# A graph-network kernel whose layer 2 changes its order of rows: products turn two columns, and the scatters move from the layer's input and its first output to its second

## The chip, the cores and the metric

The kernel runs on one core of a Trainium2 chip. The metric is the device time of one execution in microseconds. Three runs of the kernel before gave 706.58, 708.85 and 709.79 us, a median of 708.85.

## The reference

Four graph layers work on 2708 nodes with 128 features each. The adjacency matrix `adj` is sparse: its entries are 0 or between 0.05 and 1, some 9 in a row. Each layer's result is added to its input and normalised.

```python
x = _layernorm(x + _L0_gnn_ref(x, adj, adj, L0_gnn_W, L0_gnn_a))
x = _layernorm(x + _L1_gnn_ref(x, adj, L1_gnn_W, L1_gnn_b))
x = _layernorm(x + _L2_gnn_ref(x, adj, L2_gnn_W, L2_gnn_a))
x = _layernorm(x + _L3_gnn_ref(x, adj, L3_gnn_msg_w, ..., L3_gnn_ln_b))

# layer 1
A_t = A + jnp.eye(n);  D_inv = A_t.sum(axis=1) ** -0.5
return relu((D_inv[:, None] * A_t * D_inv[None, :]) @ (H @ W.T + b))
# layer 2: attention with 4 heads; what is not 1 is masked by -1e9 times its distance from 1
e = (s_i[:, None, :] + s_j[None, :, :]) * scale + ((1.0 - adj) * -1e9)[:, :, None]
out = jnp.einsum('ijh,jhd->ihd', jax.nn.softmax(e, axis=1), xp)
# layer 3
messages = gelu(s[:, None, :] + d[None, :, :] + msg_b)
aggregated = jnp.einsum('ijd,ij->id', messages, adj)
h = gelu(concat([x, aggregated]) @ upd_w.T + upd_b) + x      # then a layernorm of its own
```

With the mask of layer 2 only a row's diagonal and its largest other entry can have a share in the softmax. Layer 3 needs, for every row, all its entries with their columns.

## The kernel before

Rows lie on 128 partitions in 22 blocks (`NB`). There are two orders of rows. In the natural order block b holds rows 128b to 128b+127. In the order of degree the longest rows come first, so that block b needs only `CAPS[b]` slots, from 21 down to 2, 187 in all. `PERM` holds the row at each place, `RANK` the place of each row. `V` holds each row's entries from the largest down, and `LIDX` their columns, both in the order of degree: `V[:, :, 0]` and `LIDX[:, :, 0]` are the largest entry off the diagonal and its column.

The layers before. Layers 0 and 1 stream the dense matrix and multiply it on PE (L753) in two halves each; `search` steps on DVE fill `V` and the indices meanwhile. At the end of layer 1's first half `end1` calls `in_order_of_rows` once. It splits a column table into three bf16 parts (L305 to L309), spreads them over `BLOCK` into `back_b` (L511, one buffer), multiplies by the one-hot `BACK` in 22 small matmuls (L516), and adds up (L520): a table in the order of degree comes out in natural order. It does so for `DS`, which gives `dinv`; then DVE multiplies `H2` by it in two halves (L894), and `H2` is the weight of the second half's products.

The generator `finish` closes groups of four blocks of a layer, spread over the steps of the loop: transposes (L635), activations and residual (L641 to L649), the norm's sums on POOL (L251 to L263), squares and norm on ACT (L257, L267), transposes (L664), a copy, products with `W2` (L678), a copy into `XP` (L684). Then it stores `TA` (the features and one score, for gathering, an ACT queue DMA), and one POOL scatter per block sends whole rows of `XD` (266 words: x, features, scores, the diagonal and degree `DD`) to their places by degree in the DRAM tensor `TS` (L693, 22 scatters).

Layer 2 works in the order of degree in four sets of 6, 6, 6 and 4 blocks. POOL gathers for each block the row of the largest entry's column from `TA` (`ga`, L918, 22 gathers); SP loads `TS` back as `OWN` (L922). `own_scores`, `shares` and `rows2` are DVE work on a set, `squares` and `rows3` ACT and PE work, `roots` DVE. `rows3` gives `yd`, the "d" of layer 3, and 22 POOL scatters (L1052) send it to natural order in `TD`, by `PERM`. `norm3` (L1061) gives `X3`, the layer's output, in the order of degree, which is what layer 3 works in.

Layer 3 goes through the blocks by `TURN`. `gathers` issues one POOL gather per slot from `TD` (L1150, 187 of them) into `G`, which has four buffers. `terms` makes PE's s terms from `X3`; `diagonals` (ACT) makes diagonal matrices of the entries; `messages` adds (DVE, L1179) and applies GELU (ACT); `update` multiplies (PE, L1143). `conditions` is a set of DVE checks that run before the first `terms` on DVE and PE. `X3B` is `X3` plus a bias row (L1097).

What sets the order: each engine has one in-order queue. `pinned(...)` chains the instructions of an engine in the order of the program's text; where it is absent a scheduler may move them. The issue of the indirect DMAs, of gathers and scatters alike, is work of POOL's queue.

Of the kernel before, what the change touches and what calls it, by code (L numbers as in the profile page):

```python
# [24 lines left out]
F32 = mybir.dt.float32  # L25
# [11 lines left out]
P = 128  # L37
# [32 lines left out]
def sparse_path(  # L70
# [130 lines left out]
    LIDX = const.tile([P, NB, SLOTS], U32, name="LIDX")  # L201
    PERM = const.tile([P, NB], U32, name="PERM")
    PERMF = const.tile([P, NB], F32, name="PERMF")

    RANK = const.tile([P, NB], U32, name="RANK")

# [388 lines left out]

    HS = lists.tile([P, NB, D], F32, name="HS")
    TA = dram.tile([NP, D + HEADS], F32, name="TA")
    TS = dram.tile([NP, W_], F32, name="TS")
    H2 = lists.tile([P, NB, D], F32, name="H2")
    with (  # L600
        tc.tile_pool(name="l_nat", bufs=NAT) as nat,
# [26 lines left out]
        def finish(layer, bs, sT):  # L628


            n = len(bs)
            g = slice(bs[0], bs[-1] + 1)
            o = pt.tile([P, BANK], F32, name="o_ps")
            for j in range(n):
                pinned(T_.transpose(o[:, blk(j)], sT[:, blk(j)], ident))  # L635
            yield
            if layer:
                y = sb.tile([P, 4, D], F32, name="y1")
                for j, b in enumerate(bs):

                    pinned(V_.scalar_tensor_tensor(  # L641
                        y[:, j, :], H2[:, b, :], 1.0, o[:, blk(j)], ALU.mult, ALU.add
                    ))
                for j, b in enumerate(bs):
                    pinned(S_.activation(
                        y[:, j, :], y[:, j, :], AF.Relu, scale=dinv[:, b : b + 1]
                    ))
            for j, b in enumerate(bs):
                pinned(V_.scalar_tensor_tensor(  # L649
                    X[:, b, :], y[:, j, :] if layer else o[:, blk(j)],  # L650
                    1.0 if layer else RZ[:, b : b + 1], X[:, b, :], ALU.mult, ALU.add,
                    accum_out=SUM[:, b : b + 1],
                ))
            squares, norm = norm_sums(bs)
            yield
            yield
            squares()
            yield
            yield
            norm()  # L660
            yield
            o = pt.tile([P, BANK], F32, name="o_ps")
            for j, b in enumerate(bs):
                pinned(T_.transpose(o[:, blk(j)], X[:, b, :], ident))  # L664
            yield
            xt = small.tile([P, BANK], F32, name="xt")
            pinned(S_.copy(xt[:, : n * P], o[:, : n * P]))
            yield
            if layer:

                K = D + 2 * HEADS
                ts = []
                for k in range(0, n, 2):
                    m = min(2, n - k)
                    t = pt.tile([P, BANK], F32, name="q_ps")[:, : 2 * K]
                    ts.append((k, m, t.rearrange("p (b k) -> p b k", k=K)))
                    for i in range(m):
                        pinned(T_.matmul(  # L678
                            ts[-1][2][:, i, :], xt[:, blk(k + i)], W2, start=True, stop=True
                        ))  # L680
                yield
                for k, m, t in ts:
                    b = bs[0] + k
                    pinned(S_.copy(XP[:, b : b + m, :], t[:, :m, :]))  # L684
                yield
                yield
                nc.scalar.dma_start(
                    TA[bs[0] * P : (bs[-1] + 1) * P, :].rearrange("(b p) c -> p b c", p=P),
                    XP[:, g, : D + HEADS],
                )  # L690

                for b in bs:
                    i = G_.indirect_dma_start(  # L693
                        TS, bass.IndirectOffsetOnAxis(ap=RANK[:, b : b + 1], axis=0),
                        XD[:, b, :], None,
                    )
                    tc.declare_no_dep(i.ins, group="TS", reason="each row has a place of its own")
                    tc.add_to_no_dep_group("TS", i.ins)
            else:

                t = pt.tile([P, BANK], F32, name="q_ps").rearrange("p (b k) -> p b k", k=D)
                for i in range(n):
                    pinned(T_.matmul(t[:, i, :], ONES, B1, start=True, stop=False))
                    pinned(T_.matmul(t[:, i, :], xt[:, blk(i)], W1, start=False, stop=True))
                yield
                pinned(S_.copy(H2[:, g, :], t[:, :n, :]))
                nc.scalar.dma_start(
                    TH[bs[0] * P : (bs[-1] + 1) * P, :].rearrange("(b p) d -> p b d", p=P),
                    H2[:, g, :],
                )  # L710
            yield
# [161 lines left out]
        for h in range(2):  # L873
# [13 lines left out]
            def end1():  # L887
                if later_half:
                    return
                for _ in passes:  # L890
                    pass
                in_order_of_rows(pt, dinv, DS)
                for g in (slice(0, NB // 2), slice(NB // 2, NB)):
                    pinned(V_.tensor_tensor(  # L894
                        H2[:, g, :], H2[:, g, :],
                        dinv[:, g].unsqueeze(2).to_broadcast([P, NB // 2, D]), ALU.mult,
                    ))
# [5 lines left out]

    TD = dram.tile([NP, D], F32, name="TD")
    late = ctx.enter_context(tc.tile_pool(name="late", bufs=1))
    OWN = late.tile([P, NB, W_], F32, name="OWN")
    X3 = late.tile([P, NB, D], F32, name="X3")
    with (
        tc.tile_pool(name="l2", bufs=1) as one,
        tc.tile_pool(name="l2b", bufs=2) as sb,  # L910
# [4 lines left out]
        for k, bs in enumerate(sets):  # L915
            ga = gas[k] = one.tile([P, len(bs), D + HEADS], F32, name=f"ga{k}")
            for i, b in enumerate(bs):
                pinned(G_.indirect_dma_start(  # L918
                    ga[:, i, :], None, TA, bass.IndirectOffsetOnAxis(ap=LIDX[:, b, 0:1], axis=0)
                ))  # L920
        for k, bs in enumerate(sets):
            nc.sync.dma_start(  # L922
                OWN[:, bs[0] : bs[-1] + 1, :],
                TS[bs[0] * P : (bs[-1] + 1) * P, :].rearrange("(b p) c -> p b c", p=P),
            )
        XO = OWN[:, :, :D]
        PO = OWN[:, :, D : 2 * D]
        SJ = OWN[:, :, 2 * D : 2 * D + HEADS]
# [15 lines left out]
        pinned(S_.copy(WC, t[:, :D]))  # L944

        AM = one.tile([P, NB, 2], F32, name="AM")
        pinned(V_.tensor_scalar(AM[:, :, 1], V[:, :, 0], 1.0, MASK, ALU.subtract, ALU.mult))
        E = one.tile([P, NB, 2, HEADS], F32, name="E")
        mid = [None] * len(sets)

# [90 lines left out]
        def rows3(k):  # L1041
# [4 lines left out]
            for lo, m, z in zs:  # L1046
                for i in range(m):
                    pinned(S_.activation(  # L1048
                        yd[:, lo + i, :], z[:, i, :], AF.Copy, scale=t[:, 3, lo + i : lo + i + 1]
                    ))  # L1050
            for i, b in enumerate(bs):
                i = G_.indirect_dma_start(  # L1052
                    TD, bass.IndirectOffsetOnAxis(ap=PERM[:, b : b + 1], axis=0), yd[:, i, :], None
                )
                tc.declare_no_dep(i.ins, group="TD", reason="each row has a place of its own")
                tc.add_to_no_dep_group("TD", i.ins)

        def norm3(k):
            zs, t = mid[k]
            for i, b in enumerate(sets[k]):  # L1060
                pinned(S_.activation(  # L1061
                    X3[:, b, :], XO[:, b, :], AF.Identity, bias=t[:, 0, i : i + 1],
                    scale=t[:, 3, i : i + 1],
                ))

# [4 lines left out]
        for k in range(last + 1):  # L1070
            rows2(k)
            if k < last:
                shares(k + 1)
            squares(k)
            if k:
                roots(k - 1)
                rows3(k - 1)
        roots(last)
        rows3(last)
        for k in range(last + 1):  # L1080
            norm3(k)

# [2 lines left out]
    with (  # L1087
# [6 lines left out]
    ):  # L1094
        X3B = one.tile([P, NB, D], F32, name="X3B")
        pinned(V_.tensor_tensor(W3[:, D : 2 * D], W3[:, :D], WD, ALU.add))
        pinned(V_.tensor_tensor(X3B, X3, LN_B.unsqueeze(1).to_broadcast([P, NB, D]), ALU.add))  # L1097

        def conditions():

# [2 lines left out]
            count = one.tile([P, NB], F32, name="count")  # L1103
            for b in range(NB):
                pinned(V_.tensor_reduce(count[:, b : b + 1], has[:, b, : CAPS[b]], AX.X, ALU.add))
            pinned(V_.tensor_tensor(count, count, OWN[:, :, W_ - 1], ALU.not_equal))
            pinned(V_.tensor_reduce(FL[:, 4:5], count, AX.X, ALU.max))

            odd = one.tile([P, NB], F32, name="odd")
# [6 lines left out]


            gap = one.tile([P, NB], F32, name="gap")
            pinned(V_.tensor_tensor(gap, V[:, :, 0], OWN[:, :, W_ - 2], ALU.max))
            pinned(V_.tensor_tensor(gap, gap, V[:, :, 1], ALU.subtract))  # L1120
            pinned(V_.tensor_scalar(gap, gap, 4e-7, None, ALU.is_lt))
            pinned(V_.scalar_tensor_tensor(gap, PERMF, float(N), gap, ALU.is_lt, ALU.mult))
# [42 lines left out]
        def diagonals(k):  # L1165
# [3 lines left out]
            W = Ws[k] = wp.tile([P, CAPS[0] + 1, P], F32, name="W")  # L1169
            for s in range(n):  # L1170
                pinned(S_.activation(W[:, s, :], ident, AF.Copy, scale=V[:, b, s : s + 1]))  # L1171
            pinned(S_.activation(W[:, n, :], ident, AF.Copy, scale=OWN[:, b, W_ - 2 : W_ - 1]))

        def messages(k):
            n = CAPS[TURN[k]]
# [79 lines left out]
                tc.add_to_no_dep_group("OUT", i.ins)  # L1255

        gathers(0)
        conditions()
        terms(0)
        diagonals(0)  # L1260
# [538 lines left out]
```

## Time and profile before

| what | value |
|---|---|
| median of 3 runs | 708.85 us |
| the profiled execution, its own time | 709.3 us |
| its span, first to last instruction | 707.5 us |
| busy: PE, DVE, POOL, ACT | 451.2, 393.0, 378.5, 272.4 us |
| mean granted TensorE clock | 0.766 |
| gathers for layer 3 (L1150) | 187, first at 428.80, last at 682.74 us |
| scatters by row (L693, L1052) | 22 of 982 ns and 22 of 1102 ns on POOL |

A group's row gives line, engine, operation, output and input tiles, count, then busy time and the mean of one in ns, then the idle time ahead of it and what ended it. A timeline row gives start and duration in us, and in brackets the idle time of that engine ahead of it and its releaser. For POOL's indirect DMAs the duration is that of making the descriptors; the data land later.

### The profile page before, as it was taken

How to read it: one execution, taken by the hardware profiler on the slowest of the kernel's cores; microseconds unless marked ns; L12 is line 12 of the kernel's file. 1: busy time of each engine (PE TensorE's matmuls, PEld its weight loads, DVE VectorE, ACT ScalarE, POOL GpSimd, SP SyncE). 2: the span in 40 equal slices, each digit the busy share in tenths (PEclk: the TensorE clock that was granted, in tenths of full speed). 3: DMA queues.
4: the chain of work that ended last, by engine and by line, in shares of the span. 5: the costliest groups of instructions: out<-in, count | busy, mean ns of one | idle time of the engine just before them, and what ended most of it. 6: DMA issues, size and time to landing. Idle time of an engine off the chain costs nothing.

```text
span 707.5 us, 8193 instructions
## 1 busy us (share of the span) xinstructions
PE 451.2 (64%) x2565; PEld 301.7 (43%) x2565; DVE 393.0 (56%) x1138; ACT 272.4 (38%) x719; POOL 378.5 (53%) x449
## 2 busy tenths in 40 slices
PE   5889999996164999997511502066646546747461
PEld 5745445663152444464311501055536435545451
DVE  4767999999983856640208834111171251434466
ACT  3145655772330100174411574055335424444330
POOL 7002001221246776036577677777777777777761
PEclk9579999998556999999755555566776857788665
DMA  9968999996294999875254111222122122211210
GB/s 296 406 245 309 415 415 379 324 374 224 101 386 153 419 418 415 311 216 191 85 181 128 42 52 40 53 54 52 52 53 55 53 53 53 53 52 52 54 48 13
DMA packets 44400, 128.68 MB, mean 182 GB/s; under 512 B 7983, under 2 KB 19523, under 8 KB 38716
## 3 DMA queue, kind: packets, MB, share of 16 engines
q0 software_dynamic: 16832, 75.13, 30.2%
q1 hardware_dynamic: 21116, 49.66, 19.7%
q10 hardware_dynamic: 6400, 3.29, 1.7%
q8 instruction: 22, 0.36, 0.2%
q14 instruction: 30, 0.25, 0.1%
HBM read 119.29 MB, written 8.81 MB: 181 GB/s over the span
## 4 chain that ended last, share of the span: by engine, by line
DVE 27%; POOL 24%; PE 19%; issue 14%; DMA 9%; ACT 6%; SPq 0%; POOLq 0%; DVEq 0%; ACTq 0%
POOL G L1150 17%; PE acc L753 12%; DVE IX L580 9%; DVE cand L565 5%; DMA G<-TD,LIDX 4%; PE z L753 3%; POOL ga L918 2%; DMA TOP<-in_high 1%; POOL TS L693 1%; ACT squares L257 1%; PE w_ps L355 1%; ACT XD L267 1%; ACT X L1061 1%; DMA nat<-in_adjo,PERM 1%; POOL ln_r L262 1%
## 5 line engine op out<-in xcount | busy, mean ns | idle before, releaser
L1150 POOL DMA_INDIRECT G<-TD,LIDX x187 | 177.4, 948 | 58.7 <-issue 52.4
L1143 PE MATMUL aT_ps<-W,M 128*128 128x128 f32 x418 | 91.0, 394 | 112.5 <-ACT M L1180 105.1
L1143 PEld LDWEIGHTS aT_ps<-W,M 128*128 128x128 f32 x418 | 80.9, 292 | 126.4 <-ACT M L1180 114.0
L1179 DVE TENSOR_TENSOR M<-G,sd_ps 128x1152 f32<-128x1152 f32 (+11 forms) x22 | 28.3, 1287 | 159.0 <-DMA G<-TD,LIDX 142.8
L753 PE MATMUL acc<-ah,XD 128*128 128x512 f32 (+1 forms) x264 | 113.7, 568 | 1.0 <-ACT XD L626 1.0
L580 DVE FIND_INDEX8 IX<-V,nat 128x8 uint32<-128x2707 f32 x33 | 97.8, 2970 | 0.0
L830 ACT ACTIVATE sign<-ah 128x1536 bf16<-128x1536 f32 (+1 forms) x44 | 57.7, 1327 | 37.1 <-issue 26.8
L753 PE MATMUL acc<-ah,HS 128*128 128x512 f32 x132 | 63.3, 615 | 12.1 <-ACT HS L866 12.1
L753 PEld LDWEIGHTS acc<-ah,XD 128*128 128x128 f32 x264 | 47.9, 196 | 44.5 <-issue 41.4
L536 POOL DMA_INDIRECT nat<-in_adjo,PERM x22 | 21.5, 979 | 81.5 <-DVE IX L580 55.4
L1171 ACT ACTIVATE W<-TAB,V 128x128 f32<-128x128 f32 x187 | 56.8, 390 | 0.0
L558 DVE MAX8 V<-nat 128x8 f32<-128x2707 f32 x12 | 35.7, 2976 | 26.6 <-DMA nat<-in_adjo,PERM 26.6
L1180 ACT ACTIVATE M<-sd_ps 128x128 f32<-128x128 f32 x22 | 6.1, 278 | 113.2 <-DVE M L1179 113.2
L753 PEld LDWEIGHTS acc<-ah,HS 128*128 128x128 f32 x132 | 25.4, 196 | 44.7 <-issue 29.3
L866 ACT ACTIVATE HS<-HS,DS 128x128 f32<-128x128 f32 x22 | 8.4, 399 | 78.0 <-DMA HS<-TH,PERM 48.8
L565 DVE MAX8 cand<-nat 128x8 f32<-128x338 f32 (+3 forms) x88 | 34.3, 461 | 2.8 <-DMA nat<-in_adjo,PERM 2.8
L251 POOL TENSOR_SCALAR ln_a<-SUM 128x4 f32<-128x4 f32 (+1 forms) x12 | 2.9, 238 | 61.1 <-DVE XD L649 33.2
L1250 POOL DMA_INDIRECT out_x<-yo,PERM x22 | 22.1, 1003 | 18.5 <-DVE yo L1229 11.3
L861 POOL DMA_INDIRECT HS<-TH,PERM x22 | 21.0, 957 | 19.6 <-DMA TH<-H 10.1
L1052 POOL DMA_INDIRECT TD<-yd,PERM x22 | 24.2, 1102 | 9.6 <-ACT yd L1048 4.1
L753 PE MATMUL acc<-ah,H 128*128 128x512 f32 (+1 forms) x88 | 28.1, 462 | 0.0
L693 POOL DMA_INDIRECT TS<-XD,RANK x22 | 21.6, 982 | 11.3 <-issue 5.4
(281 smaller groups left out, 862.6 us busy)
## 6 DMA issues: line engine op xcount, KB each, us to landing
ah<-in_adjL SPq DMA_DIRECT2D x22, 768.0 KB, 13.5
ah<-in_adjR SPq DMA_DIRECT2D x44, 330.0 KB, 5.5
TOP<-in_high SPq DMA_DIRECT2D x5, 1354.0 KB, 13.0
ah<-in_adjL SPq DMA_DIRECT2D x22, 256.0 KB, 7.2
G<-TD,LIDX POOLq DMA_INDIRECT x187, 2.5
OWN<-TS SPq DMA_DIRECT2D x3, 798.0 KB, 8.5
TA<-XD ACTq DMA_DIRECT2D x5, 264.0 KB, 2.8
TH<-H ACTq DMA_DIRECT2D x5, 256.0 KB, 10.2
```

What stands on the lines that cost most here:

```text
L558: pinned(nc.vector.max(V[:, b, 0:8], t))
L565: pinned(nc.vector.max(c[:, 8 * k : 8 * k + 8], t[:, at]))
L580: pinned(nc.vector.max_index(IX[:, b, s], V[:, b, s], t))
L693: i = G_.indirect_dma_start(TS, bass.IndirectOffsetOnAxis(ap=RANK[:, b : b + 1], axis=0), XD[:, b, :], None,)
L753: pinned(T_.matmul(acc[i][:, :w], weights[:, n, :], a[:, i * BANK : i * BANK + w], start=n == 0, stop=n == NB - 1,))
L830: pinned(S_.activation(m[:, : hi - lo], a, AF.Sign))
L1052: i = G_.indirect_dma_start(TD, bass.IndirectOffsetOnAxis(ap=PERM[:, b : b + 1], axis=0), yd[:, i, :], None)
L1143: pinned(T_.matmul(t, a, b, start=n == 0, stop=n == len(parts) - 1))
L1150: pinned(G_.indirect_dma_start(G[:, s, :], None, TD, bass.IndirectOffsetOnAxis(ap=LIDX[:, b, s : s + 1], axis=0),))
L1171: pinned(S_.activation(W[:, s, :], ident, AF.Copy, scale=V[:, b, s : s + 1]))
L1179: pinned(V_.tensor_tensor(M[:, :n, :], G[:, :n, :], s_, ALU.add))
L1250: i = G_.indirect_dma_start(out, bass.IndirectOffsetOnAxis(ap=PERM[:, b : b + 1], axis=0), h, None, bounds_check=N - 1, oob_is_err=False,)
```

## The change

Layer 2 works in natural order, directly on `XD`. The scatter into `TS` and the load of `OWN` go. For the gather and the mask, `V[:, :, 0]` and `LIDX[:, :, 0]` are turned into natural order as `V1` and `J1` by two more calls of `in_order_of_rows`. `d` is stored by four plain SP DMAs. The layer's output `X3N`, with the diagonal and degree in two more columns, is scattered to places by degree into `XS` (22 POOL scatters) and loaded back as `X3S` by four SP loads. Four of the scatters, the loads, the sum `X3B` and the conditions come behind `gathers(0)` in the text.

```diff
@@ end of finish(1) @@
-                for b in bs:
-                    i = G_.indirect_dma_start(
-                        TS, bass.IndirectOffsetOnAxis(ap=RANK[:, b : b + 1], axis=0),
-                        XD[:, b, :], None,
-                    )
...
@@ end1 @@
                 in_order_of_rows(pt, dinv, DS)
+                in_order_of_rows(pt, V1, V[:, :, 0])
+                jf = small.tile([P, NB], F32, name="jf")
+                pinned(V_.tensor_copy(jf, LIDX[:, :, 0]))
+                js = small.tile([P, NB], F32, name="up")
+                in_order_of_rows(pt, js, jf)
+                pinned(V_.tensor_copy(J1, js))
...
@@ layer 2 @@
-    OWN = late.tile([P, NB, W_], F32, name="OWN")
-    X3 = late.tile([P, NB, D], F32, name="X3")
+    OWN = XD
+    X3N = late.tile([P, NB, D + 2], F32, name="X3N")
+    X3S = late.tile([P, NB, D + 2], F32, name="X3S")
+    X3 = X3S[:, :, :D]
+    XS = dram.tile([NP, D + 2], F32, name="XS")
+
+    def to_places(bs):
+        for b in bs:
+            i = pinned(G_.indirect_dma_start(
+                XS, bass.IndirectOffsetOnAxis(ap=RANK[:, b : b + 1], axis=0), X3N[:, b, :], None
+            ))
...
+    def from_places():
+        for bs in groups(6):
+            nc.sync.dma_start(
+                X3S[:, bs[0] : bs[-1] + 1, :],
+                XS[bs[0] * P : (bs[-1] + 1) * P, :].rearrange("(b p) c -> p b c", p=P),
+            )
...
-                    ga[:, i, :], None, TA, bass.IndirectOffsetOnAxis(ap=LIDX[:, b, 0:1], axis=0)
+                    ga[:, i, :], None, TA, bass.IndirectOffsetOnAxis(ap=J1[:, b : b + 1], axis=0)
...
-        for k, bs in enumerate(sets):
-            nc.sync.dma_start(
-                OWN[:, bs[0] : bs[-1] + 1, :],
-                TS[bs[0] * P : (bs[-1] + 1) * P, :].rearrange("(b p) c -> p b c", p=P),
-            )
+        pinned(V_.tensor_copy(X3N[:, :, D:], DD))
...
-            for i, b in enumerate(bs):
-                i = G_.indirect_dma_start(
-                    TD, bass.IndirectOffsetOnAxis(ap=PERM[:, b : b + 1], axis=0), yd[:, i, :], None
-                )
+            nc.sync.dma_start(
+                TD[bs[0] * P : (bs[-1] + 1) * P, :].rearrange("(b p) d -> p b d", p=P),
+                yd[:, : len(bs), :],
+            )
...
             if k:
                 roots(k - 1)
                 rows3(k - 1)
+            if k > 1:
+                norm3(k - 2)
+                to_places(sets[k - 2])
         roots(last)
         rows3(last)
-        for k in range(last + 1):
+        for k in (last - 1, last):
             norm3(k)
+        to_places(sets[last - 1])
...
@@ layer 3 @@
         gathers(0)
+        to_places(sets[last])
+        from_places()
+        pinned(V_.tensor_tensor(X3B, X3, LN_B.unsqueeze(1).to_broadcast([P, NB, D]), ALU.add))
         conditions()
         terms(0)
         diagonals(0)
```

In the built program POOL's queue holds, behind the 22 gathers of layer 2: 19 scatters into `XS`, the 21 gathers of `gathers(0)`, 3 scatters, and the rest of the gathers. PE's queue holds the three sets of 22 small matmuls behind each other, with the remaining products of layer 1's first half behind them.

## The prediction

> **What bounds the kernel now.** I read the page's shares and groups first. From 429 us to the end POOL's gathers are back to back, and layer 3 waits for them:
>
> ```profile
> DVE 27%; POOL 24%; PE 19%; issue 14%; DMA 9%; ACT 6%; SPq 0%; POOLq 0%; DVEq 0%; ACTq 0%
> L1150 POOL DMA_INDIRECT G<-TD,LIDX x187 | 177.4, 948 | 58.7 <-issue 52.4
> ```
>
> The idle time ahead of them is "issue", 0.3 us for each: one gather every 1.25 us, 187 of them 234 us. The list of waits says who suffers:
>
> ```profile
> DVE M L1179 <- DMA G<-TD,LIDX: 142.8, 17, 23.7
> ```
>
> So any shift of POOL's stream goes one to one into the end, while a shift of DVE, ACT or PE in layer 3 is free within the slack of four G buffers. The question is only when POOL gets through its work. POOL's timeline around layer 2:
>
> ```profile
> 361.64 0.96 POOL L693 DMA_INDIRECT TS<-XD,RANK  x1 [0.30 <-issue]
> 362.90 1.00 POOL L918 DMA_INDIRECT ga<-TA,LIDX  x1 [0.30 <-issue]
> ...
> 392.01 0.94 POOL L918 DMA_INDIRECT ga<-TA,LIDX  x1 [0.30 <-issue]
> 396.11 1.00 POOL L1052 DMA_INDIRECT TD<-yd,PERM  x1 [3.15 <-ACT yd L1048]
> ...
> 423.52 3.23 POOL L1052 DMA_INDIRECT TD<-yd,PERM  x1 [0.30 <-DMA TD<-yd,PERM]
> 428.80 1.29 POOL L1150 DMA_INDIRECT G<-TD,LIDX  x1 [2.05 <-DVE odd L1110]
> ```
>
> POOL idles 3.15 us before the TD scatters, and 2.05 at their end, where the first gather needs the last scatter landed. The last scatter took 3.23 us instead of 0.96, because DVE ran this from 422.83 to 425.92:
>
> ```profile
> 422.83 3.09 DVE L1097 TENSOR_TENSOR X3B<-X,LN_B 128x2816 f32<-128x2816 f32 x1 [11.35 <-ACT X L1061]
> ```
>
> Last, PE in layer 1's second half, which POOL's TS scatters hold up (ln_v and ln_m stand behind four of them in POOL's queue, ACT's norm waits for ln_m, and PE's transpose for ACT):
>
> ```profile
> 297.59 0.86 PE L516 MATMUL q_ps<-back_b,BACK 128*128 128x66 bf16 x22
> ...
> 300.94 2.38 PE L753 MATMUL acc<-ah,H 128*128 128x512 f32 x8
> ...
> 324.23 1.54 PE L664 MATMUL o_ps<-TAB,XD 128*128 128x128 f32 x4 [2.49 <-ACT XD L267]
> 325.57 4.06 PE L753 MATMUL acc<-ah,H 128*128 128x512 f32 x8
> ...
> 333.03 1.48 PE L664 MATMUL o_ps<-TAB,XD 128*128 128x128 f32 x4 [1.36 <-ACT XD L267]
> ```
>
> **The change, part by part.** I work with the times of the profiled execution (709.3 us, 0.45 above the median of the runs) and follow the start of the first ga gather, A, which is 362.9 before.
>
> *1. Two more products in end1.* back_b has one buffer, so each call must wait for the matmuls of the one before, and PE's queue stands meanwhile, with the rest of the first half's products behind. First call: matmuls end at 298.45, as now (PE, not DVE, is late there; DVE waited 5.8 us for it, so splitting V1 earlier is free). Then DVE: L520 0.3, three L511 at 0.66 (1.8 overlapped): 300.6. PE 0.9: 301.5. DVE: L520 and the cast of LIDX 0.5; the whole split and spread took 290.01 to 292.67, 2.7: 304.7. PE 0.9: 305.6. DVE: L520 and the cast to J1 0.5, H2's first half 1.6: 307.7. PE meanwhile does the six products that lay between 298.29 and 300.94, 2.65: 308.3. The second half starts at 308.3 instead of 300.94: **+7.3**.
>
> *2. TS scatters gone from POOL.* Third group: its squares end at 318.6, ln_v could run then and not at 321.99; PE's idle 2.49 goes and its transposes need 0.6, not 1.5: -3.35. Fourth group likewise: squares done near 324.2 (shifted), the norm ready before PE gets there: the 1.36 and the 0.9 of stretched transposes, -2.2. Fifth group: ln_a waited for eight scatters until 344.63, its sum was ready near 343.4: -1.2. Together **-6.75**. Last, six scatters stood ahead of ga until 362.6, though TA had landed at 358.32 + 1.75 = 360.1: ga can start at 360.2, **-2.7**.
>
> *The clock, where a rule speaks against part 1.* Behind PE's gap of 2.49 us the profile's stretches give a granted clock of 0.88 from 324 to 326 and 0.50 from 326 to 328, and eight products took 4.06 us where they take 2.38: 1.7 us lost. The Trainium skill, "TensorE: Matmul & The Clock Gate", Part 1 (The HAM clock gate), says the clock halves after an idle window of about 3.4 us. Part 1's gaps are 2.2 and 3.2 us, split by a burst: by the rule alone they might pass free; by the row I charge 1.7 for them. The gap at 321.7 goes, with its own slow stretch: -1.5. By the rule +0 and -1.5, by the row +0.2, which I take. A = 360.2 + 7.3 - 6.75 + 0.2 = **361.0**.
>
> *3. Layer 2 up to the first XS scatter.* OWN is no longer loaded: own_scores (waited for 369.64 to 376.78) runs before ga lands, and the set waits for its gathers. The last gather of set 2 lands at A+26.5 (before 391.23, A+28.3: OWN's loads delayed early landings to 5.5 us, later ones were 2.5 to 4.6; 17 pitches of 1.25, 2.1 of contention, 3.1 landing). The DVE stretch from E of set 2 to E of set 3 was 391.35 to 399.50, 8.15: A+34.7. From there to the end of yd of set 1 was 399.50 to 405.2, 5.7: A+40.4. Only behind it on ACT's queue stands norm3(0) (0.49 for one), then a release of 0.36: first scatter at A+41.2 = **402.2**. Before it was yd of set 0, one set earlier, that released POOL at 396.11. POOL's last ga ends near A+29.7, so it idles some 11 us instead of 3.
>
> *4. POOL from there.* 22 XS scatters cost what 22 TD scatters cost (0.96 + 0.30 each, 27.8 together); the 187 gathers are the same. Before, 428.80 - 396.11 = 32.7 us passed until the first gather, 4.9 more than 27.8. After, the first gather waits for no scatter: TD's stores go by SP (free by then; 2.8 us each by the TA row of the same size), the last near A+50, landed by 414, and POOL reaches its first gather near 426. ACT delivers X3N of sets 1 and 2 near A+46 and A+50.5, when POOL is at its 7th (A+48.8) and 13th (A+56.4): hidden. What stays is X3B, now beside gathers. The row says 2.3 us lost. The skill's "Trainium Architecture — The Big Picture", What this means for kernel authors, calls the port that DVE and GpSimd share "an exclusive lock", which would cost up to 3.1, and also the full 0.95 for each sum in layer 2, where the trace shows gathers of 1.33 for 0.94, 0.39 lost. I take the rows, and 0.4 for the sums of the conditions: 2.7. In terms of the first gather: 402.2 + 27.8 + 2.7 = 432.7 against 428.8: **+3.9 us**.
>
> *5. Late consumers.* The 22nd XS scatter ends at 402.2 + 19x1.265 + 21x1.25 + 3x1.265 = 456.3, lands 2.3 later; SP's four loads take perhaps 9 (OWN's, of twice the bytes in as many rows, took 12 for all): 467. Then X3B 3.1, conditions 8.2, PE and ACT 2: the first add near 481 instead of 457.9; gelu must wait for 6.2 us of diagonals that were early before: 487 instead of 460.8. Cover: POOL needs the first G buffer back for its 58th gather, near 504; slack 20 us. ACT's own turns took 11.2, 8.4, 7.6 (460.84 to 472.1, 475.7 to 484.1, 490.56 to 498.1) against POOL's 16.3, 15, 13.8: the lag is made up by the fifth turn; the first stores to out come in the seventh. Costed at nothing; without this cover it would be up to 26 us.
>
> *6. At nothing:* V1, J1, the copy of DD and jc on DVE (before ga lands). SP's from_places stops nothing: its queue is empty behind it.
>
> Sum: A comes 1.9 earlier (+7.3 - 6.75 - 2.7 + 0.2), the first scatter stands 8.0 further behind A (41.2 for 33.2), and 2.2 of wait and lock go (2.7 for 4.9): **+3.9**, 713.2 on the profiled 709.3, 712.8 on the median of 708.85; I say **713**. Break-even is A near 357.
>
> **The rivals.**
> *No change that can be told (within 0.5%, 3.5 us).* The same mechanism with part 1 a little cheaper (2 us if H2 or DVE overlaps better) or ga landing in 2.6. 711. For it: +3.9 lies close to the bound. Chance 0.34.
> *Faster.* PE's gaps in end1 are hidden or the freed POOL speeds layer 1's tail more than I see: the place is A. If the products cost nothing, A is 353.8 and the end 3.3 us earlier, 705.5; it decides where A falls below 353.6 (0.5%). Against: the one back_b buffer and PE's order force the chain, so this needs also an earlier norm3(0). Chance 0.09.
> *Much slower.* The late X3S breaks the cover of part 5: the first add ends after 504, and POOL's gathers stop for a buffer, all that is over 504 being paid. It would need the loads of XS 20 us later. 720 and up. Chance 0.07, within slower.
> *The change doesn't do what it says* at one place: only three of the last four scatters stand behind gathers(0). Worth 1.3 us of lag, nothing at the end.
>
> **How the numbers follow.** Slower by over 0.5% has the forecast's upper part (0.49) and the broken cover: 0.56; within 0.34; faster 0.10. The unknown ends: end1 5.5 to 8.5, clock -1.5 to +2, landing 2.6 to 4.6, the lock 0 to +1, the runs' spread 3 us. That is +3.9 with -6 and +6 or so: 706.5 to 719. The range of slower alone is 712.4 to 719.
>
> **What would show it.** After: two gaps of PE near 299 and 303, the second half's products starting near 308; no idle of PE ahead of L664 near 324 and 333; A near 361; POOL idle some 11 us before the first XS, which ACT's norm3 releases; no wait ahead of the first G gather; a gather of about 3 us where X3B runs; the first add near 481, the adds back on DMA by the fifth turn; the last gather near 686.6. It is wrong if A is below 357, if the first scatter comes within 38 us of A, or if any gather waits for DVE's M.

## The result, and the profile after

On the chip of the first runs the changed kernel takes 712.82 us (median of 7 runs, 712.31 to 715.31) and the kernel before 708.13 (7 runs, 706.30 to 709.79): a ratio of 1.0071, 95% interval 1.0055 to 1.0087. So it is slower, by a little. Predicted were 713.0 and a range of 706.5 to 719. The profiled execution took 712.5 us, its span is 710.5 (709.3 and 707.5 before).

The largest group on the page of the changed kernel, and the line of the list of waits that answers to the one before:

```profile
L1167 POOL DMA_INDIRECT G<-TD,LIDX x187 | 179.7, 961 | 57.0 <-issue 52.1
```

```profile
DVE M L1196 <- DMA G<-TD,LIDX: 98.7, 17, 11.2
```

Layer 3 is still bound by POOL's gathers. DVE waits 98.7 us for them instead of 142.8: its first add now comes 22 us later and finds its gathers landed, and as no gather waits for an add, that costs nothing here. TensorE's timeline at the end of layer 1's first half and in the second half:

```profile
298.03 0.86 PE L519 MATMUL q_ps<-back_b,BACK 128*128 128x66 bf16 x22
300.93 0.87 PE L519 MATMUL q_ps<-back_b,BACK 128*128 128x66 bf16 x22 [2.04 <-DVE back_b L514]
304.91 1.39 PE L519 MATMUL q_ps<-back_b,BACK 128*128 128x66 bf16 x22 [3.11 <-DVE back_b L514]
306.11 3.34 PE L747 MATMUL acc<-ah,HS 128*128 128x512 f32 x4
...
310.14 2.38 PE L747 MATMUL acc<-ah,H 128*128 128x512 f32 x8
...
335.98 1.11 PE L666 MATMUL o_ps<-TAB,XD 128*128 128x128 f32 x4
```

There are the two waits for DVE's lists, then a third product of 1.39 us instead of 0.87, and the second half begins at 310.14 instead of 300.94. The last row is one of the transposes of L666: from 312 to 340 none of them waits any more, now that the scatters of TS are gone. POOL's timeline:

```profile
363.74 1.10 POOL L938 DMA_INDIRECT ga<-TA,J  x1 [7.22 <-issue]
...
404.19 1.00 POOL L915 DMA_INDIRECT XS<-X3N,RANK  x1 [10.62 <-ACT X3N L1075]
...
428.44 0.98 POOL L1167 DMA_INDIRECT G<-TD,LIDX  x1 [0.30 <-issue]
...
468.61 2.84 POOL L1167 DMA_INDIRECT G<-TD,LIDX  x1 [0.30 <-issue]
...
688.67 0.97 POOL L1167 DMA_INDIRECT G<-TD,LIDX  x1 [0.30 <-issue]
...
706.03 0.98 POOL L1267 DMA_INDIRECT out_x<-yo,PERM  x1 [1.06 <-DVE yo L1258]
```

POOL waits 10.62 us for the first X3N (3.15 for the first yd before); nothing holds the first G gather; one gather takes 2.84 us. The last gather is issued at 688.67 instead of 682.74, and the last store of the output at 706.03 instead of 702.44. DVE's two rows that belong to this:

```profile
467.54 3.09 DVE L1277 TENSOR_TENSOR X3B<-X3S,LN_B 128x2816 f32<-128x2816 f32 x1 [57.42 <-DMA X3S<-XS]
...
480.22 2.96 DVE L1196 TENSOR_TENSOR M<-G,sd_ps 128x2688 f32<-128x2688 f32 x1 [1.46 <-PE sd_ps L1160]
```

### The profile page after: what moved, and what is told of

It is laid out like the page before. It is cut to its first block, busy times and chain, and to the rows that moved or that the text cites. A ratio compares the mean times of both kernels' runs of the same rounds, so it can differ in the third digit from the quotient of the medians.

```text
span 710.5 us, 8271 instructions
## 1 busy us (share of the span) xinstructions
PE 442.8 (62%) x2609; PEld 294.3 (41%) x2609; DVE 398.2 (56%) x1159; ACT 271.3 (38%) x719; POOL 357.5 (50%) x427
## 4 chain that ended last, share of the span: by engine, by line
DVE 27%; POOL 23%; PE 19%; issue 13%; DMA 12%; ACT 5%; SPq 1%; POOLq 0%; DVEq 0%; ACTq 0%
POOL G L1167 17%; PE acc L747 12%; DVE IX L583 9%; DVE cand L568 5%; DMA G<-TD,LIDX 4%; DMA TOP<-in_high 3%; PE z L747 3%; POOL ga L938 2%; POOL XS L915 2%; ACT squares L260 1%; ACT XD L270 1%; DVE XD L651 1%; DMA nat<-in_adjo,PERM 1%; POOL ln_r L265 1%; DVE M L1196 1%
## 5 line engine op out<-in xcount | busy, mean ns | idle before, releaser
L1167 POOL DMA_INDIRECT G<-TD,LIDX x187 | 179.7, 961 | 57.0 <-issue 52.1
L1160 PE MATMUL aT_ps<-W,M 128*128 128x128 f32 x418 | 82.5, 366 | 80.5 <-ACT M L1197 73.1
L1160 PEld LDWEIGHTS aT_ps<-W,M 128*128 128x128 f32 x418 | 73.1, 266 | 93.1 <-ACT M L1197 80.8
L1196 DVE TENSOR_TENSOR M<-G,sd_ps 128x1152 f32<-128x1152 f32 (+11 forms) x22 | 28.3, 1287 | 109.0 <-DMA G<-TD,LIDX 98.7
L1277 DVE TENSOR_TENSOR X3B<-X3S,LN_B 128x2816 f32<-128x2816 f32 x1 | 3.1, 3091 | 57.4 <-DMA X3S<-XS 57.4
L938 POOL DMA_INDIRECT ga<-TA,J x22 | 23.4, 1065 | 13.6 <-issue 13.3
```

The source lines that it names most:

```text
L938: pinned(G_.indirect_dma_start(ga[:, i, :], None, TA, bass.IndirectOffsetOnAxis(ap=J1[:, b : b + 1], axis=0)))
L1160: pinned(T_.matmul(t, a, b, start=n == 0, stop=n == len(parts) - 1))
L1167: pinned(G_.indirect_dma_start(G[:, s, :], None, TD, bass.IndirectOffsetOnAxis(ap=LIDX[:, b, s : s + 1], axis=0),))
L1196: pinned(V_.tensor_tensor(M[:, :n, :], G[:, :n, :], s_, ALU.add))
```

## The experiments

The experiments fell on four chips, and that has to be known to read them. On chip A the kernel before takes 707.5 us; on chips B, C and D it takes 789.0, 788.2 and 794.1, and layer 3 is not bound by POOL there. The record of the result above names no chip; the kernel before took 708.1 there, and I count it with A. From set 1 (below) to the first G gather the changed kernel and its variants with the same stages agree to a few tenths on A, B and D (130.4, 130.4 to 130.8, 130.3 us). I therefore compare stages across chips, by distances within one trace, and whole times only on one chip.

These distances carry most of what follows (us; "set 1" is the start of the first 22 matmuls of end1, the same place in all kernels):

| kernel | set 1 to second half | set 1 to first ga | first ga to first scatter of TD or XS |
|---|---|---|---|
| before | 3.35 | 65.31 | 33.21 |
| changed | 12.11 | 65.71 | 40.45 |
| e1, without the products | 3.35 | 56.63 | 40.34 |
| e2, before with the products | 12.46 | 74.49 | 31.64 |
| e5, with the TS scatters | 12.49 | 74.57 | 41.42 |
| e9, gaps filled | 10.25 | 63.59 | 40.43 |
| e4, lists first | 4.75 | 58.09 | 40.27 |
| e3, norms early | 12.52 | 65.74 | 32.21 |

**What the products cost: e1 and e2.** The changed kernel loses them, the kernel before gets them.

```
-                in_order_of_rows(pt, V1, V[:, :, 0])
-                jf = ...; in_order_of_rows(pt, js, jf)
-                pinned(V_.tensor_copy(J1, js))
+                pinned(V_.tensor_copy(V1, V[:, :, 0]))
+                pinned(V_.tensor_copy(J1, LIDX[:, :, 0]))
```

> The changed kernel without its two extra products: V1 and J1 are plain copies of V's and LIDX's first columns, which leaves out turning them into natural order (the outputs are then of other neighbours). Theory (the products stop TensorE, and all behind the first half of layer 1 follows): the second half's products start near 301.4 instead of 310.14, no matmul in the first half runs at half clock, the first ga gather goes out near 355.0 instead of 363.74, and the time is 8 to 9 us below the changed kernel's 712.8: about 704. Rival (the products are covered, and the growth comes from the scatters of X3N): the second half moves, the end does not, 712 to 713.

Measured on chip A: 703.99 us, ratio to before 0.9954 (0.9942 to 0.9966), 8.8 less than the changed kernel, or 8.2 if each is taken against the kernel before that ran beside it. TensorE's timeline of e1, behind set 1 at 296.38:

```profile
297.08 1.96 PE L747 MATMUL acc<-ah,HS 128*128 128x512 f32 x4
...
299.73 2.38 PE L747 MATMUL acc<-ah,H 128*128 128x512 f32 x8
```

The six products behind set 1 follow at once and take 2.65. The second half starts 8.8 us sooner after set 1, and the first ga gather 9.1 sooner. The products are not covered.

> The kernel before with the two extra products added and their results read by nobody. Theory: the second half's products start near 310 instead of 300.94, the scatters of TS and their stalls of TensorE stay as they are and only shift, and the time is 8 to 9 us above 708.1: about 716.5. Rival (the stalls that TS puts on TensorE take up the delay, since POOL's scatters then have more time): plus 0 to 4, 708 to 712.

Measured on chip A: 714.74 us, ratio 1.0097 (1.0075 to 1.0118), 7.2 more than before. The larger stall of TensorE behind the TS scatters is there as before (2.49 us ahead of one transpose). The smaller one shrinks from 1.36 to 0.44, but eight products behind the larger take 4.61 us instead of 4.06. The first ga gather comes 9.2 later after set 1, so the stalls take up nothing in the end, and the rival fails at that place. Of the 9.2, 1.6 are given back in layer 2, perhaps because OWN's loads have more time, and 2.5 in the tail, of which more below. That puts the time under what I expected.

**What the removal of TS was worth: e5.** The 22 scatters stand again where they stood, and nobody reads TS.

> The changed kernel with the 22 scatters of TS put back on POOL where they stood; their result is read by nobody. Theory (their removal was worth 8 to 10 us in the second half of layer 1: 6.6 in TensorE's waits ahead of L664/L666, the rest in front of the ga gathers): the idle ahead of o_ps comes back, the first ga gather goes out 8.5 to 10.5 us later, near 373, and the time is 8 to 10 us above the changed kernel's 712.8, less up to 2.5 that the tail may give back: 719 to 722. Rival (POOL has more idle time in that stage than the scatters need, so their removal saved little): 713 to 716.

Measured on chip B: 801.65 us, ratio to before 1.0220 (1.0139 to 1.0301). The changed kernel has no run on that chip, so whole times cannot be compared, but the stage can be read. TensorE and POOL of e5:

```profile
333.96 1.63 PE L667 MATMUL o_ps<-TAB,XD 128*128 128x128 f32 x4 [2.48 <-ACT XD L270]
```

```profile
372.76 1.00 POOL L947 DMA_INDIRECT ga<-TA,J  x1 [0.30 <-issue]
```

The wait of 2.48 ahead of a transpose is back, six scatters stand ahead of ga again, and set 1 to ga grows from 65.71 to 74.57: 8.9 us, within the theory. e2 and e1 say the same from the other side: 74.49 - 65.71 = 8.8 is the removal in a kernel with the products, 65.31 - 56.63 = 8.7 in one without. Products and removal thus cancel: +9.2 - 8.8, and 0.4 is left at ga.

**Waits, clock and matmuls of the products: e9 and e4.** e9 puts matmuls that nobody reads into the two gaps:

```
                 in_order_of_rows(pt, dinv, DS)
+                filled(pt, 44)          # 128x66, bf16, BACK by itself
                 in_order_of_rows(pt, V1, V[:, :, 0])
+                filled(pt, 70)
```

> The changed kernel with matmuls that nobody reads (44 and 70 of 128x66, bf16) in TensorE's two waits for DVE between the three products, so that TensorE is busy there; everything else is as it was. Theory (the halved clock of 303 to 308 comes from those two waits of 2.0 and 3.1 us): the third product takes 0.87 and not 1.39, the remaining six products of the first half 2.7 and not 4.0, and the second half starts 1.7 to 2.0 us earlier, near 308.3; the time is 0.5 to 2 us lower. Rival (the clock falls for another reason, or waits of this length do not matter to it): the second half starts where it did, near 310.1, or later.

Measured on chip B: 788.96 us, ratio to before 1.0012 (0.9989 to 1.0035); without a run of the changed kernel beside it the whole time says little. The trace says it plainly. The profile's stretches from 302 to 303 and from 306 to 308 of the changed kernel, and then the latter of e9; the granted clock is the third number from the end (from 303 to 306 it is 0.50 and 1.00):

```profile
302.00:303.00 1.00, 0.00 (x0) 0.00 (x0) 0.93 (x5) 0.00 (x0) 0.00 (x0) 0.53 0.00 0
306.00:308.00 2.00, 2.00 (x9) 0.97 (x7) 1.63 (x3) 0.00 (x0) 0.00 (x0) 0.50 0.00 0
```

```profile
306.00:308.00 2.00, 2.00 (x6) 0.89 (x6) 1.90 (x3) 0.73 (x2) 0.00 (x0) 1.00 0.00 0
```

and TensorE's timeline of e9:

```profile
305.15 0.87 PE L526 MATMUL q_ps<-back_b,BACK 128*128 128x66 bf16 x22 [0.98 <-DVE back_b L521]
...
308.52 2.38 PE L754 MATMUL acc<-ah,H 128*128 128x512 f32 x8
```

With the gaps filled, the clock stays at 1.00, the third product takes 0.87 instead of 1.39 and the six products 2.66 instead of 4.03. The second half starts 10.25 after set 1 instead of 12.11 (12.3 to 12.5 in the other kernels of chip B): 1.9 to 2.3 us were the clock. The waits for DVE themselves stay: the second and third set start 2.90 and 6.88 us after set 1 in both kernels.

e4 removes both: all three lists are made first, in back_b and in two buffers of layer 0 that are free by then, and 66 matmuls follow one another.

```
-                in_order_of_rows(pt, dinv, DS)
-                in_order_of_rows(pt, V1, V[:, :, 0])
-                ...
+                in_order_of_rows(pt, signs, (dinv, DS), (V1, V[:, :, 0]), (js, jf))
```

> The changed kernel with the three products in one row: the parts and the lists of all three (three buffers in place of one) are made on DVE before the first of them, where DVE waits for TensorE anyway, and the 66 matmuls follow one another. Theory (what the products cost is TensorE's waits for DVE and the halved clock behind them, not the matmuls): the three sets of 22 take 0.87 each without a gap, the remaining six products 2.65 instead of 4.03, the second half starts near 303 instead of 310.1, and the time is near 706 (6 to 7.5 us less than 712.8). Rival (the matmuls and reductions themselves cost, or the clock halves for another reason): the second half starts after 307, and the time is 710 to 713.

Measured on chip A: 705.11 us, ratio 0.9962 (0.9947 to 0.9977), 7.1 to 7.7 less than the changed kernel. TensorE of e4:

```profile
297.19 0.86 PE L526 MATMUL q_ps<-back_b,BACK 128*128 128x66 bf16 x22
297.89 1.55 PE L526 MATMUL q_ps<-sign,BACK 128*128 128x66 bf16 x44
299.29 1.96 PE L757 MATMUL acc<-ah,HS 128*128 128x512 f32 x4
```

No gap; the second half starts 4.75 after set 1. Of the 8.8 us, 1.4 are the matmuls themselves, 7.4 were one buffer and the order of the instructions. The prediction saw that DVE waits there anyway and counted V1's split as free; e4 shows that all three lists fit into that time once each has a buffer.

**POOL's idle time before XS: e3.**

```
             if k:
                 roots(k - 1)
                 rows3(k - 1)
-            if k > 1:
-                norm3(k - 2)
-                to_places(sets[k - 2])
+                norm3(k - 1)
+                to_places(sets[k - 1])
```

and the last set's scatters stand ahead of the first gathers.

> The changed kernel with the norms of a set written directly behind that set's rows of yd (not one set later), each set's scatters directly behind them, and all 22 scatters of X3N ahead of the first G gather. Theory (the 10.6 us in which POOL waits for the first X3N are a price on the path): the first XS scatter goes out near 396 instead of 404.2, the scatters run on at 1.275 us each, the last G gather and the end come 7 to 8.5 us earlier: about 705. Rival 1 (the last set's rows bound the first G gather, through TD): the first gather waits for TD's landing and the end moves by under 2 us. Rival 2 (the earlier norms on ScalarE delay the next set's squares, and so the last set): gain under 4 us.

Measured on chip A: 705.09 us, ratio 0.9968 (0.9953 to 0.9984), 7.1 to 7.7 less than the changed kernel. POOL of e3:

```profile
395.65 1.17 POOL L915 DMA_INDIRECT XS<-X3N,RANK  x1 [2.58 <-ACT X3N L1075]
...
424.13 0.99 POOL L1165 DMA_INDIRECT G<-TD,LIDX  x1 [0.30 <-issue]
```

The idle time falls from 10.62 to 2.58, first ga to first scatter from 40.45 to 32.21, and the first gather, now behind all 22 scatters, waits for nothing. Both rivals fail: TD had landed, and ScalarE's earlier norms delayed nothing that counts.

**The cover of the late consumers: e6, e7 and f2.** Gathers of later blocks (13, and 25) stand ahead of the last four scatters of X3N.

```
-        gathers(0)
+        for k in range(m + 1):          # m = 1 in e6 and f2, 2 in e7
+            gathers(k)
         to_places(sets[last])
```

> The changed kernel with the second block's 13 gathers moved ahead of the last four scatters of X3N, so that X3S, X3B and the first message add come some 16.5 us later (near 497) while POOL's list of work is as long as before. Theory (the late consumers of X3S are covered, because the fifth block's gathers, which need the first G buffer back, begin only near 505): no change, 712 to 713.5, with the first add near 497. Rival (any delay of the first add is paid at the end, since DVE and ACT run behind the gathers from there on): 5 to 16 us slower.

> As in the case before, but with the second and the third block's gathers (25 in all) ahead of the last four scatters, so that the first add comes some 32 us later, near 512 to 515, behind the moment (near 505) at which POOL wants the first G buffer back. Theory: POOL's first stall in the gathers, 8 to 12 us ahead of the fifth block, and the end later by about that, 720 to 724. Rival 1 (the buffers' slack is larger than the count of them says): no change. Rival 2 (every delay is paid): 30 us slower.

Measured on chip B: 796.14 and 799.22 us, ratios 1.0124 (1.0056 to 1.0192) and 1.0170 (1.0102 to 1.0238). Neither can decide about chip A: POOL stops for DVE's adds on chip B without the edit too (45.7 us in e9). e9, with its filled gaps, took 788.96 there with its first add at 509.55, e6 and e7 7.2 and 10.3 us more with theirs at 518.65 and 519.14, so some lateness is paid on B. But the changed kernel itself was missing, so it and e6 were run once more on one chip.

> The changed kernel itself, beside the kernel before and beside the two kernels that follow, on one chip. The last five runs fell on two chips on which the kernel before takes 788 to 789 us instead of 707.5, because TensorE waits in layer 3 for no cause that the trace shows, 2 to 17 us at a time. If this chip is one of the quick ones: ratio to before 1.007, as at first. If it is one of the slow ones, the gathers do not bound layer 3 there; theory: the ratio is then 1.003 to 1.012, since the first G gather is as late (428.4 against 428.8) but the first message add is 22 us later and is no longer covered.

> The second block's 13 gathers ahead of the last four scatters of X3N, once more, now beside the changed kernel. Quick chip: theory (16 us more of lateness of the first add are covered by the fifth block's gathers beginning only near 505): the same time as the changed kernel within 0.2%; rival (any delay is paid): 5 to 16 us slower. Slow chip, where the consumers and not the gathers bound layer 3: theory: the 16 us are paid in part or whole, 8 to 16 us above the changed kernel; rival (still covered): within 0.3%.

Both fell on chip D: 793.29 us, ratio 0.9987 (0.9961 to 1.0013), and 800.33, ratio 1.0086 (1.0056 to 1.0117). There the first add comes at 510.31 and 517.46. X3B starts 17.0 us later in f2, but the conditions behind it take 10 us less, so that 7.15 are left, and the times are 7.04 apart. In this one pair the lateness is paid in full. POOL of f1, the changed kernel, shows what differs from chip A:

```profile
513.53 0.94 POOL L1167 DMA_INDIRECT G<-TD,LIDX  x1 [9.20 <-DVE M L1196]
```

POOL waits six times, 50.0 us in all, for a G buffer that DVE's add must free. On chip A the same kernel has no such wait. That 16 us more would still be free on chip A was not measured; it stays read from the trace, not shown. My expectation for the ratio on such a chip, 1.003 or more, was wrong: the change costs nothing there that can be told. Why the kernel before is as slow there has no trace, and stays open.

**Both gains together: e8 and f3.** e3's and e4's edits in one kernel.

> The two edits that gained, together: the lists of all three products first (7.7 us less than the changed kernel), and the norms and scatters of X3N one set earlier (7.7 us less). Theory (the two lie in different stages of one path): they add up, 697 to 698.5, which is 1.4% below the kernel before; first ga gather near 355.3, first scatter of X3N near 387, last G gather near 673. Rival (with both, something else is late, such as TD in front of the first gather, or the adds of the messages): 701 to 705.

> The two gaining edits together, once more. Quick chip: 697 to 698.5, ratio to before 0.985 to 0.987, 2.1% below the changed kernel. Slow chip: 0.98 to 0.985 of before, as measured on the first slow one. Rival (the two gains overlap): no better than either edit alone, 0.996.

Measured: 774.07 us on chip C, ratio 0.9832 (0.9792 to 0.9872); 776.73 on chip D, ratio 0.9799 (0.9776 to 0.9823), 16.6 us less than the changed kernel there. It beats the kernel before on both chips, and the changed kernel on D. Its stages up to the scatters add up as they should, on chip D 58.11 from set 1 to ga and 32.41 from ga to the first scatter, each as in e4 and e3 alone. On chip A it was not run: the 697 to 698.5 us expected there are an estimate from 712.8 less twice 7.7. Why it gains as much where POOL is not the bound stays open.

## Why the prediction was right, step by step

**1, the products.** Right. Predicted +7.3 and 1.7 for the clock; e1 and e2 measure 8.8 and 9.1 at the second half and 9.1 to 9.2 at ga. On the clock the row was right: gaps of 2.04 and 3.11 us, with 0.87 us of matmuls between them, gave 0.50 from 303 to 308, and e9 shows that without them it stays at 1.00. But the two gaps are not alike. The 0.53 from 302 to 303 puts the fall at 302.06, when the second gap was only 0.26 us old. So it was the first gap, with these 0.26 us, that brought the clock down, and the rest of the second can only have kept it there. It came back near 308.9 (0.78 from 308 to 310), after 6.8 us. In the kernel before it was down from 325.5 to 329.0 (0.88 from 324 to 326, 0.76 from 328 to 330), 3.4 us. These are two and one of the windows of about 3.4 us that the Trainium skill states ("TensorE: Matmul & The Clock Gate", Part 1, The HAM clock gate: the clock halves after an idle window). So the trace agrees with the window's length; but the 3.4 us ahead of the two falls held 1.1 and 1.3 us of matmuls and transposes, so a window need not be idle throughout.

**2, the removal of TS.** The mechanism was right, the size was not. With the slow stretch that goes with it, I had -6.75 - 2.7 - 1.5 = -10.95; e5 measures -8.9. The failed term is "ga can start at 360.2": 1.75 for TA to land and 0.1 to start. The chain of waits of the changed kernel, just ahead of the first ga gather at 363.74:

```profile
360.15 2.27 DMA TA<-XD
```

TA's last store took 2.27 and POOL started 1.32 after it had landed: 3.59 instead of 1.85, 1.7 of the 2.1 us that were missing. Before, six scatters stood over this time, so no row of POOL before showed how soon it can follow a store. Also, DVE's sums of own_scores now run beside POOL's last ln_m, which takes 0.87 us there instead of 0.19. So A was 363.74 and not 361.0.

**3, layer 2.** Right: A + 40.45 (predicted 41.2), released by ACT's X3N, with 10.62 us of idle time (11).

**4, POOL from there.** Right: from the first scatter to the last gather 284.48 us instead of 286.63, 2.15 less (2.2 predicted), with no wait at the first gather. X3B cost 1.9 us on one gather, where the row had 2.3. But the prediction was wrong to set its rows against "an exclusive lock" (the skill's "Trainium Architecture — The Big Picture", What this means for kernel authors): the rows agree with it. The gather began 1.07 us after X3B and ended 0.82 after X3B's end; before, the scatter began 0.69 after X3B and ended 0.83 after its end. Likewise every gather of layer 2 that began during one of DVE's sums of two tiles ended 0.81 or 0.82 after the sum, in both kernels. So POOL's instruction stood until the sum was over, and its loss depends only on how soon after the sum's start it began: 1.9 us here, 2.5 in e3 and e4, 0.2 to 0.7 beside the sums of 0.95. Neither 3.1 nor 0.95 is due in full, and that 2.3 and 0.4 came near was luck.

**5, the late consumers.** Right on chip A: X3B at 467.54 (467), first add at 480.22 (481), no gather that waits for an add, and an add that waits for its gathers again, 11.21 us, in the fifth turn. On the other chips POOL does stop for a G buffer, as the rival of the broken cover had it; but the kernel before takes as long on D as the changed one, so the change does not pay for it there.

**The sum.** +5.9 us at the last gather, where +3.9 was predicted; 0.4 of it is there before end1. But the end moved by only 3.6, because the tail gave back 2.3 us. So the two misses cancel, and that the measured time lies so near the 713 is luck. The tail was not in my sum. DVE before, then after:

```profile
674.52 0.29 DVE L1206 TENSOR_TENSOR yo<-yo,X 128x128 f32<-128x128 f32 x1 [1.97 <-ACT yo L1196]
...
684.00 0.81 DVE L1179 TENSOR_TENSOR M<-G,sd_ps 128x640 f32<-128x640 f32 x1
```

```profile
678.35 0.28 DVE L1223 TENSOR_TENSOR yo<-yo,X3S 128x128 f32<-128x128 f32 x1
...
687.58 0.81 DVE L1196 TENSOR_TENSOR M<-G,sd_ps 128x640 f32<-128x640 f32 x1
```

The last add but one stands on DVE behind the norms of a set, which begin with this yo; the end follows it by 18.4 us in both kernels. Before, yo waited 1.97 us for ScalarE; after, the wait is gone, because DVE's add ahead of it came later. From the last gather to the last store it is 19.7 us before and 17.4 after, and 18.9 in e1, 18.5 in e3 and e4. e2, with the order of the kernel before, has 17.2: so the shorter tail does not hang on the new order; how gathers and adds fall against each other would explain it, which was not tested. "One to one into the end" holds to about 2.5 us only.

## What to carry to other kernels

A product that waits for another engine's preparation costs the preparation and, where the gaps halve the clock, what runs behind them: make all operands first, in buffers that are free, and let the matmuls follow one another (1.4 us instead of 8.8 here). When a scattered store leaves a queue, ask which transfer it had covered, for that wait appears next; and when it moves behind a later result, look whether that result can be made one set sooner (7.1 to 7.7 us here). What a DVE sum of two tiles costs POOL depends on where POOL's next instruction falls, not on a fixed price. Cover that rests on a bound of one engine is cover only where that engine is the bound.

## What the runs showed of the hardware that was not expected

On three of four chips the kernel before takes about 80 us more, and so does the changed kernel on D, the only one of the three on which it was run. Its trace f1 agrees with that of chip A up to the first G gather, so all of it lies in layer 3. The instructions do not take longer (DVE is busy for 398.1 us in f1 and 398.2 on A), but many start late, with "issue" or "remote" as what ended the wait, and neither names an engine. By far the most is lost ahead of ACT's copy of the aggregated rows, for which PE and DVE then wait in turn. The line of f1's waits, and one of the seven with POOL and PE beside it:

```profile
ACT aT L1207 <- remote: 83.4, 7, 27.8
```

```profile
630.47 0.95 POOL L1167 DMA_INDIRECT G<-TD,LIDX  x1 [0.30 <-issue]
636.26 0.27 ACT L1207 COPY aT<-aT_ps 128x128 f32<-128x128 f32 x1 [27.80 <-remote]
636.58 0.80 PE L1160 MATMUL f_ps<-UB,aT 128*128 128x128 f32 x2 [26.73 <-ACT aT L1207]
```

On A this copy waits 20.1 us in all, at most 2.8 at a time, and for PE. Here PE, DVE and ACT had finished by 610.2, and until 636.26 only POOL's gathers ran. In six of the seven waits the copy starts 1.4 to 4.8 us after the last of a row of gathers, while POOL stands still. That the gathers hold ACT up is a guess from this, and no run tests it.

DVE and PE are late too. From X3B's start to the first add it is 43.6 us in f1 and 12.7 on A. Many starts on both engines stand 1.4, 2.1 or 2.8 us apart, where the instructions take 0.2 to 0.4. No run here shows the cause of either, and it stays open.
